# An LSTM kernel: a 256 KB reload split by partitions, and weight rows in DRAM reordered for strided stores

## The chip, the cores and the metric

One core of a Trainium2 chip. The metric is device time in microseconds of one execution; the kernel before is given by three runs with their median. Besides there is one profiled execution, whose own time is shown beside its span.

Engines in the text: PE (TensorE: matrix products; PEld its weight loads), DVE (VectorE), ACT (ScalarE), POOL (GpSimd), SP (SyncE, here only an issuer of DMAs). SPq and ACTq are the instruction queues of SP and ACT when they issue DMAs. Sixteen DMA engines carry out what both issue.

## What is computed

An LSTM over 512 steps with batch 32 and 512 hidden units, and its hidden states added to the input:

```
xW = einsum('ntd,dg->ntg', x, Wx) + b          # x: (32, 512, 512), Wx: (512, 2048)
for each step t:
    a = xW[:, t] + h @ Wh                      # Wh: (512, 2048)
    i, f, o = sigmoid(a[:, :512]), sigmoid(a[:, 512:1024]), sigmoid(a[:, 1024:1536])
    g = tanh(a[:, 1536:])
    c = f * c + i * g
    h = o * tanh(c)
    out[:, t] = x[:, t] + h
```

All in float32. The steps are sequential; `x @ Wx` is not.

## The kernel before

**Layout.** A step's gates stand as 128 partitions x 512 columns: partition `32 j + b` has block j of the hidden units for batch row b, and the 512 columns are two halves (`HW` = 256) of four gates x 64 units. `bank_of(t)` is the PSUM bank in which step t's gates are summed.

**A step** (the loop over `t`, line 779). `h_part(t)` puts `h @ Wh` into the bank: 16 products of 512 columns, which PE carries out as 32 matmul instructions (line 214). Then `cell(t)`: ACT takes the sigmoids and tanh (lines 228 to 230), DVE multiplies and adds (231 to 235), ACT takes tanh of c (237), DVE forms h and transposes it (239, 245) for the next step; POOL adds x (250) and SP stores pairs of steps (254). While the cell runs, PE works on `x @ Wx` of later steps. The bank of step t+1 is filled ahead by `seed_step` (line 591): ACT copies the ready `xW` rows from `xw`, a ring of three tiles, into the bank. `load_xw(t + 3)` reloads that ring from DRAM, from `kept` (line 575, steps 5 to 23) or from `xwd` (line 580, all groups): 128 partitions x 512 columns, 256 KB, by one DMA whose source is read with the index j outermost.

**The stream.** Steps 0 to 23 (the head) get their `xW` by plain products (`plain_block`, line 162), and so do the last 8. The 480 steps between are done in 20 groups of 24 steps, by a scheme with fewer products: sums of blocks of x (`u_op`, line 394) times sums of blocks of Wx, 20 slots a group, each slot with seven products `r` of a 2x2 scheme, each product four matmuls (line 483). Results are collected from PSUM by `evacuate` (ACT 529, 538, 545; DVE 535, 539, 542), combined by `w_op` (DVE 359) and stored to `xwd` in DRAM (`store_blocks`, line 375), from which the reload takes them. The work of a step is fixed when the program is made: 560 matmuls a group over 24 steps.

**Weight rows.** The sums of Wx blocks are the same for all groups. In the head DVE makes them: `tail_sums` once (lines 611 to 614), then `v_add` per slot (line 631) into one of six buffers, and `v_store` (line 645) sends them to `vdram` in DRAM. In `vdram`, row n holds the seven weight blocks (128 partitions x 256 columns each) that the stream uses together. They belong to different slots: `ROW` lists product and delay, so `(6, 1)` means that row n has product 6 of slot n-1. `RIGHT` gives a product's place in the row, `LEFT` its place among the x blocks. A slot's sum is thus spread over the rows s to s+3, and row numbers are taken modulo 20. `load_v` (line 557; 560 and 563 for the first and last rows) brings one row of 896 KB into `vring`, a ring of three, and `load_v_ahead` keeps two rows ahead of the products.

**Order.** The schedule is written by hand, and each engine's queue runs in that order. On SP a step has: the output store (which waits for POOL), the `xwd` stores (which wait for DVE), every eighth step a load of x, the `xw` reload, the rows of `vring` (which wait for PE to be done with the ring's place), and once per group `load_group` (1.5 MB of x). On ACT, in the head, the stores of `v_store` are issued in `flush_v`, after `cell(t)` and ahead of `seed_step(t + 1)`.

`late_load` (line 169) brings Wx back for the last 8 steps; `_laid_out` orders the inputs in memory before the run.

Of the kernel before, what the change touches and what calls it, by code (L numbers as in the profile page):

```python
# [7 lines left out]
F32 = mybir.dt.float32  # L8
# [4 lines left out]
P = 128  # L13
B = 32
T = 512
NJ = 4
G = 4
TC = 8
NCHUNK = T // TC
H = P // 2  # L20
W = G * P
HW = G * H
# [5 lines left out]
R = 20  # L28
TAU = (1, 0, 2)
NS = NG * R  # L30
# [27 lines left out]
]  # L58
BIAS_OF = {1: "b3", 3: "b1-b3", 8: "b2+b3", 11: "b2-b0", 13: "b0", 17: "b1-b0"}

ROW = ((1, 0), (5, 0), (2, 0), (6, 1), (3, 1), (7, 2), (4, 3))
LEFT = {1: 0, 2: 1, 4: 2, 5: 3, 6: 4, 7: 5, 3: 6}
RIGHT = {1: 0, 2: 1, 3: 2, 5: 3, 6: 4, 7: 5, 4: 6}

FILL = 107.0
PROD = 4 * 108.0
# [22 lines left out]
def kernel(  # L89
# [10 lines left out]
    nc = tc.nc  # L100
# [4 lines left out]
    dram = ctx.enter_context(tc.tile_pool(name="dram", bufs=1, space=DRAM))  # L105
# [7 lines left out]
    r1 = const.tile([P, 8, 4, HW], F32, name="r1")  # L113
    cbuf = const.tile([P, NC, 4, HW], F32, name="cbuf")
    r2 = cbuf[:, 0:8]
    wh_sb = const.tile([P, NJ, NJ, W], F32, name="wh_sb")
    vring = const.tile([P, 3, 7, HW], F32, name="vring")
# [8 lines left out]
    bias_full = const.tile([P, W], F32, name="bias_full")  # L126
    xw = const.tile([P, 3, W], F32, name="xw")

    vdram = dram.tile([R, P, 7, HW], F32, name="vdram")
    xwd = [dram.tile([6, P, NJ, W], F32, name=f"xwd_{i}") for i in range(2)]  # L130
    kept = dram.tile([HEAD - KEPT, P, W], F32, name="kept")

# [18 lines left out]
    def plain_block(t, c, bank):  # L151

        ko, ki = divmod(c, 2)
        for j in range(NJ):
            w = raw(ko * 4 + j)
            dst = bank[j * B : (j + 1) * B]
            if ki == 1:
                pieces = [(dst, w[:, 2:4].rearrange("p s c -> p (s c)"))]
            else:
                pieces = [(dst[:, 0:HW], w[:, 1]), (dst[:, HW:W], w[:, 0])]  # L160
            for n, (d, m) in enumerate(pieces):
                nc.tensor.matmul(  # L162
                    d, x_of(t)[:, c], m, start=c == 0 and n == 0, stop=True, skip_group_check=True
                )
# [109 lines left out]
    def flat(a):  # L274
        return a.rearrange("p a b -> p (a b)")
# [276 lines left out]
    def load_v(row):  # L552

        rr = row % R
        if row >= 3:
            if row < NS:
                nc.sync.dma_start(out=vring[:, row % 3], in_=vdram[rr])
            else:
                for a in {0: 2, 1: 5, 2: 6}[row - NS],:
                    nc.sync.dma_start(out=vring[:, row % 3, a:7], in_=vdram[rr, :, a:7])  # L560
            return
        for a, b in {0: ((0, 2), (3, 4)), 1: ((0, 5),), 2: ((0, 6),)}[row]:
            nc.sync.dma_start(out=vring[:, row % 3, a:b], in_=vdram[rr, :, a:b])

    def load_v_ahead():

# [5 lines left out]
    def load_xw(t):  # L572
        dst = xw[:, t % 3]
        if t < HEAD:
            nc.sync.dma_start(out=dst, in_=kept[t - KEPT])
            return
        g, n = divmod(t - HEAD, GS)
        assert getattr(group(g), "stored", 0) >= 4 * (n // 8 + 1), (t, group(g).__dict__.get("stored"))
        m, q = divmod(n, 4)
        nc.sync.dma_start(out=dst, in_=xwd[g % 2][m, q * B : (q + 1) * B].rearrange("b j c -> j b c"))  # L580

    xw_late = {}

    def seed_step(t):
# [10 lines left out]
    vroom = [vring[:, i] for i in range(3)] + [  # L595
        ubuf[:, 2 * i : 2 * i + 2].rearrange("p a b c -> p (a b c)").rearrange("p (k c) -> p k c", k=7) for i in range(3)
    ]
    free_v = list(range(6))
    vt = {}
# [5 lines left out]
    def tail_sums(a, b):  # L605

        z, w = r1[:, a:b], r2[:, a:b]
        b12, b11, b21, b22 = (z[:, :, i] for i in range(4))
        t1, t2, t3, n4 = (w[:, :, i] for i in range(4))
        return [  # L610
            lambda: sub(t1, b12, b11),
            lambda: sub(t3, b22, b12),
            lambda: sub(t2, b22, t1),
            lambda: sub(n4, b21, t2),
        ]

    def v_parts(i):
        if i < 8:
            return r1[:, i, 1:4], r2[:, i]
        return vroom[vt[i]][:, 0:3], vroom[vt[i]][:, 3:7]  # L620

    def v_add(terms):
        (a, sa), (b, sb) = sorted(terms.items(), key=lambda v: -v[1])
        op = add if sb > 0 else sub
        dst = free_v.pop(0)
        if a > 7 and b > 7:
            op(flat(vroom[dst]), flat(vroom[vt[a]]), flat(vroom[vt[b]]))
        else:
            for n, (pa, pb) in enumerate(zip(v_parts(a), v_parts(b))):
                d = vroom[dst][:, 0:3] if n == 0 else vroom[dst][:, 3:7]  # L630
                op(flat(d), flat(pa), flat(pb))
        for i in (a, b):
            v_used(i)
        return dst
# [5 lines left out]
                free_v.append(vt[i])  # L640

    def v_store(s, parts, whole=None):
        lo, hi = parts
        to = lambda k: vdram[(s + k) % R]
        dma = lambda o, i: nc.scalar.dma_start(out=o, in_=i)
        dma(to(0)[:, 0:2], lo[:, 0:2])
        dma(to(0)[:, 3], hi[:, 0])
        if whole is None:
            dma(to(1)[:, 2], lo[:, 2])
            dma(to(1)[:, 4], hi[:, 1])  # L650
        else:
            dma(to(1)[:, 2:5:2], whole[:, 2:5:2])
        dma(to(2)[:, 5], hi[:, 2])
        dma(to(3)[:, 6], hi[:, 3])

    def v_sum(i):
        if i > 7 and i not in vt:
# [4 lines left out]
    def v_slot(s):  # L662

        terms = V_OF[s]
        for i in terms:
            v_sum(i)
        if len(terms) > 1:
            d = v_add(terms)
            v_stores.append(lambda: v_store(s, (vroom[d][:, 0:3], vroom[d][:, 3:7]), vroom[d]))
            free_v.append(d)  # L670
        else:
            (i,) = terms
            parts = v_parts(i)
            v_stores.append(lambda: v_store(s, parts, vroom[vt[i]] if i > 7 else None))
            v_used(i)

    v_stores = []
# [39 lines left out]
    with tc.manual_schedule():  # L717
# [4 lines left out]
        for c in range(4):  # L722
            ko, ki = divmod(c, 2)
            nc.sync.dma_start(
                out=r1[:, 4 * ko : 4 * ko + 4, 2 * ki : 2 * ki + 2].rearrange("p j s c -> p j (s c)"),
                in_=wx[c].rearrange("p (j c) -> p j c", j=NJ),
# [178 lines left out]
def _laid_out(name, a):  # L905
    import numpy as _np

    if name == "x":
        a = a.reshape(B, NCHUNK, TC, NJ, NJ, B).transpose(1, 3, 5, 2, 4, 0).reshape(NCHUNK, P, TC * P)
    elif name == "x_grouped":  # L910
        a = a[:, HEAD : HEAD + NG * GS]
        a = a.reshape(B, NG, 3, 2, 4, NJ, 2, 2, B)[:, :, [TAU.index(m) for m in range(3)]]
        a = a.transpose(1, 5, 8, 2, 6, 3, 7, 4, 0)
        a = a.reshape(NG, P, 3, 2, 4, 4, B)[:, :, :, :, [2, 0, 1, 3]]
        a = a.reshape(NG, P, 6 * 4 * P)
    elif name == "cond_1024":
        a = a.reshape(B, NJ, NJ, B).transpose(1, 3, 2, 0).reshape(P, P)
    elif name == "L0_cond_Wx":
        a = a.reshape(NJ, NJ, B, G, NJ, 2, H).transpose(1, 0, 2, 4, 5, 3, 6).reshape(4, P, NJ, 2, HW).copy()
        a[0::2] = a[0::2, :, :, ::-1].copy()  # L920
        a = a.reshape(4, P, NJ * W)
    elif name == "L0_cond_Wh":
        a = a.reshape(NJ, NJ, B, G, NJ, 2, H).transpose(0, 2, 1, 4, 5, 3, 6).reshape(P, NJ * NJ * W)
    else:
        a = a.reshape(G, NJ, 2, H).transpose(1, 2, 0, 3).reshape(NJ, W)
    return _np.ascontiguousarray(a)
# [25 lines left out]
```

## Time and profile before

| | |
|---|---|
| runs | 3340.66, 3340.87, 3352.6 us, median 3340.87 |
| profiled execution | 3353.58 us, its span 3351.7 us |
| granted PE clock, mean | 0.977 |
| h products (line 214, the gate banks), 16288 matmuls | 1872.6 us busy, 41.9 idle before them |
| stream products on x sums (line 483), 14400 matmuls | 1107.1 us busy, 100.2 idle before them |
| PE waiting for `vring` (longest 6.0 us) | 97.3 us, 33 times |
| ACT's line 591 waiting for `xw` (longest 4.0 us) | 94.3 us, 38 times |
| SP waiting for PE before line 557 (longest 6.0 us) | 392.6 us, 150 times |

An x after a number is a count. Share of busy time is an average over the whole span; the prediction goes by stretches of it. In a timeline a line has start, duration, engine, line of the code, operation, what is written and read, shape and count; behind it in brackets the idle time before it and what ended it. In the rows for one line of the code, the three numbers are shortest, median and longest duration in ns.

### The profile page before, as it was taken

The page shows a single profiled execution, that of the slowest core. Times are in us where ns is not written, and L with a number is a line of the kernel's source. Part 1 is how long each engine was busy: PE and PEld are TensorE (multiplying, and loading weights), DVE is VectorE, ACT ScalarE, POOL GpSimd, SP SyncE. Part 2 cuts the span into 40 slices and gives each one's busy share as a digit, 9 for nine tenths or more (in the row PEclk, how much of TensorE's full clock was granted, in tenths as well). Part 3 has the DMA queues.
Part 4 walks back from the last instruction along what each step waited for, and adds up shares of the span by engine and source line. Part 5 has one row for each costly group of instructions (what it writes and reads, how often), then busy time and mean ns, then how long its engine had stood idle before and what let it go on. Part 6 is the DMA issues. An engine that isn't in the chain of part 4 may idle for free. (4 is left out here: it accounts for less than half of the span.)

```text
span 3351.7 us, 101512 instructions
## 1 busy us (share of the span) xinstructions
PE 3193.8 (95%) x41432; PEld 1856.8 (55%) x41432; DVE 2149.2 (64%) x6749; ACT 1350.9 (40%) x4525; POOL 233.0 (7%) x508
## 2 busy tenths in 40 slices
PE   8699999999999999999999999999999999999898
PEld 5355555555556555555556565555656565556454
DVE  5367667676666767576666666575766666666544
ACT  0144434444444444344434344444434443444344
POOL 0000000000000000000000000000000000000010
PEclk9799999999999999999999999999999999999999
DMA  7577676777677677767777676777677776767721
GB/s 281 194 275 257 215 251 230 233 240 236 234 236 245 216 258 227 237 225 234 247 231 242 219 254 215 249 232 234 229 238 243 233 247 213 254 219 252 230 101 40
DMA packets 277889, 766.46 MB, mean 229 GB/s; under 512 B 20656, under 2 KB 66736, under 8 KB 276912
## 3 DMA queue, kind: packets, MB, share of 16 engines
q1 hardware_dynamic: 259936, 740.83, 67.0%
q10 hardware_dynamic: 17488, 19.14, 1.7%
q8 instruction: 327, 5.36, 0.7%
q14 instruction: 138, 1.13, 0.1%
HBM read 577.18 MB, written 182.71 MB: 227 GB/s over the span
## 5 line engine op out<-in xcount | busy, mean ns | idle before, releaser
L214 PE MATMUL gbank<-wh_sb,ht 128*32 128x512 f32 (+1 forms) x16288 | 1872.6, 589 | 41.9 <-ACT gbank L591 34.0
L483 PE MATMUL xbank<-vring,ubuf 128*32 128x256 f32 x14400 | 1107.1, 384 | 100.2 <-DMA vring<-vdram 96.6
L214 PEld LDWEIGHTS gbank<-wh_sb,ht 128*32 128x32 f32 x16288 | 714.5, 111 | 879.1 <-issue 713.1
L483 PEld LDWEIGHTS xbank<-vring,ubuf 128*32 128x32 f32 x14400 | 712.3, 111 | 375.7 <-issue 238.9
L231 DVE TENSOR_TENSOR fc<-s 128x128 f32<-128x128 f32 (+1 forms) x546 | 153.5, 281 | 985.5 <-ACT s L228 984.6
L228 ACT ACTIVATE s<-gbank 128x256 f32<-128x256 f32 (+1 forms) x509 | 191.5, 376 | 1334.0 <-PE gbank L214 1178.9
L359 DVE TENSOR_TENSOR cbuf<-cbuf 128x1024 f32<-128x1024 f32 x480 | 577.3, 1217 | 2.1
L250 POOL TENSOR_TENSOR oc<-xnat,ht 128x128 f32<-128x128 f32 x504 | 232.8, 462 | 3080.3 <-DVE ht L245 1777.8
L591 ACT COPY gbank<-xw 128x512 f32<-128x512 f32 x473 | 282.2, 597 | 136.8 <-DMA xw<-xwd 94.3
L237 ACT ACTIVATE tanh_c<-s 128x64 f32<-128x64 f32 x1024 | 210.5, 249 | 270.6 <-DVE s L235 269.7
L529 ACT COPY cbuf<-xbank 128x512 f32<-128x512 f32 x400 | 231.3, 578 | 144.7 <-PE xbank L483 134.6
L239 DVE TENSOR_TENSOR hbuf<-o,tanh_c 128x64 f32<-128x64 f32 x1024 | 193.3, 225 | 140.3 <-ACT tanh_c L237 140.0
L483 PE MATMUL bbank<-vring,ubuf 128*32 128x256 f32 x2400 | 279.9, 384 | 1.2 <-DVE cbuf L535 1.2
L483 PE MATMUL xbank<-vring,r 128*32 128x256 f32 x2400 | 221.4, 379 | 1.2 <-ACT tanh_c L237 1.2
L483 PE MATMUL xbank<-vring,xs 128*32 128x256 f32 x2400 | 217.4, 380 | 2.7 <-ACT xbank L513 1.0
L245 DVE STREAM_TRANSPOSE ht<-hbuf 128x64 f32<-128x64 f32 x1022 | 193.7, 225 | 9.0 <-DVE hbuf L239 2.0
L235 DVE TENSOR_TENSOR s<-fc,ig 128x64 f32<-128x64 f32 x1024 | 183.9, 218 | 2.3
L233 DVE TENSOR_TENSOR ig<-s 128x64 f32<-128x64 f32 x1024 | 183.5, 218 | 0.0
L535 DVE TENSOR_TENSOR cbuf<-bbank,cbuf 128x256 f32<-128x256 f32 x400 | 163.7, 409 | 9.6 <-ACT cbuf L529 6.9
L539 DVE TENSOR_TENSOR cbuf<-xbank,cbuf 128x256 f32<-128x256 f32 x400 | 161.2, 403 | 4.8 <-ACT cbuf L538 3.1
L542 DVE TENSOR_TENSOR cbuf<-xbank,cbuf 128x256 f32<-128x256 f32 x400 | 161.7, 404 | 2.8 <-PE xbank L483 2.8
L545 ACT COPY cbuf<-xbank 128x256 f32<-128x256 f32 x400 | 147.6, 369 | 33.4 <-PE xbank L483 29.0
(84 smaller groups left out, 1817.0 us busy)
## 6 DMA issues: line engine op xcount, KB each, us to landing
vring<-vdram SPq DMA_DIRECT2D x397, 896.0 KB
xwd<-cbuf SPq DMA_DIRECT2D x240, 512.0 KB
xw<-xwd SPq DMA_DIRECT2D x480, 256.0 KB
out_dram<-oc SPq DMA_DIRECT2D x255, 128.0 KB
xnat<-in_x_dram SPq DMA_DIRECT2D x63, 512.0 KB
xs<-in_x_grouped_dram SPq DMA_DIRECT2D x10, 1536.0 KB
r<-in_x_grouped_dram SPq DMA_DIRECT2D x10, 1536.0 KB
kept<-cbuf SPq DMA_DIRECT2D x19, 256.0 KB
```

The source lines that it names most:

```text
L214: nc.tensor.matmul(dst[j * B : (j + 1) * B], state["ht"][:, k], m, start=False, stop=True, skip_group_check=True)
L228: nc.scalar.activation(s[:, i, 0:2], g[:, :, 0:2], AF.Sigmoid)
L233: nc.vector.tensor_mul(ig[:, u], s[:, u, 0], s[:, u, 2])
L235: add(nxt[:, u, 3], fc[:, u], ig[:, u])
L237: nc.scalar.activation(tanh_c[:, HALVES[u]], nxt[:, u, 3], AF.Tanh)
L239: nc.vector.tensor_mul(hbuf[:, HALVES[u]], o[:, u], tanh_c[:, HALVES[u]])
L245: nc.vector.transpose(ht[:, 2 * u : 2 * u + 2].rearrange("p q b -> p (q b)"), hbuf[:, HALVES[u]])
L250: (nc.gpsimd if t < T - 8 else nc.vector).tensor_add(oc[:, tt % 2], x_of(t), ht)
L359: op(c_of(dst), c_of(src), c_of(bb))
L483: nc.tensor.matmul(dst[q * B : (q + 1) * B], left_of(gr, s, r)[:, q * B : (q + 1) * B], vring[:, row % 3, RIGHT[r]], start=start, stop=Tru ...
L529: nc.scalar.copy(t[:, 0:4:3], xb.rearrange("p (n c) -> p n c", n=2))
L591: nc.scalar.copy(bank_of(t), src)
```

## The change

Three things. The reload of `xw` from `xwd` becomes four DMAs of 32 partitions, one per block j. The products of a row are ordered by delay (`ROW`, `RIGHT`: two places of delay 0, two of delay 1, two of delay 2, one of delay 3), so that a slot's sum lies in `vdram` at a constant stride and is stored by two DMAs, or three where the sum is a plain block of Wx. For that `vdram` has three rows more instead of the wrap by modulo, and `load_v` reads the rows 0, 1 and 2 of a pass in two parts. The sums are laid out in the buffers to match: `split_parts` takes places 0, 2, 4, places 1, 3, 5 and place 6, so `v_add` has three operations where a plain block of Wx is among its terms. The halves of the Wx blocks are stored in the reverse order in memory, and `plain_block` always uses two products of 256 columns.

```diff
-ROW = ((1, 0), (5, 0), (2, 0), (6, 1), (3, 1), (7, 2), (4, 3))
+ROW = ((1, 0), (5, 0), (6, 1), (3, 1), (7, 2), (2, 2), (4, 3))
 LEFT = {1: 0, 2: 1, 4: 2, 5: 3, 6: 4, 7: 5, 3: 6}
-RIGHT = {1: 0, 2: 1, 3: 2, 5: 3, 6: 4, 7: 5, 4: 6}
+RIGHT = {1: 0, 5: 1, 3: 2, 6: 3, 2: 4, 7: 5, 4: 6}
...
-    vdram = dram.tile([R, P, 7, HW], F32, name="vdram")
+    vdram = dram.tile([R + 3, P, 7, HW], F32, name="vdram")
...
-            if ki == 1:
-                pieces = [(dst, w[:, 2:4].rearrange("p s c -> p (s c)"))]
-            else:
-                pieces = [(dst[:, 0:HW], w[:, 1]), (dst[:, HW:W], w[:, 0])]
+            pieces = [(dst[:, 0:HW], w[:, 2 * ki + 1]), (dst[:, HW:W], w[:, 2 * ki])]
...
     def load_v(row):
 
         rr = row % R
-        if row >= 3:
-            if row < NS:
-                nc.sync.dma_start(out=vring[:, row % 3], in_=vdram[rr])
-            else:
-                for a in {0: 2, 1: 5, 2: 6}[row - NS],:
-                    nc.sync.dma_start(out=vring[:, row % 3, a:7], in_=vdram[rr, :, a:7])
-            return
-        for a, b in {0: ((0, 2), (3, 4)), 1: ((0, 5),), 2: ((0, 6),)}[row]:
-            nc.sync.dma_start(out=vring[:, row % 3, a:b], in_=vdram[rr, :, a:b])
+        cut = min(2 * rr + 2, 7)
+        parts = []
+        if row < NS:
+            parts.append((rr, 0, cut))
+        if row >= R and cut < 7:
+            parts.append((rr + R, cut, 7))
+        for n, a, b in parts:
+            nc.sync.dma_start(out=vring[:, row % 3, a:b], in_=vdram[n, :, a:b])
...
-        nc.sync.dma_start(out=dst, in_=xwd[g % 2][m, q * B : (q + 1) * B].rearrange("b j c -> j b c"))
+        for j in range(NJ):
+            nc.sync.dma_start(out=dst[j * B : (j + 1) * B], in_=xwd[g % 2][m, q * B : (q + 1) * B, j])
...
-        b12, b11, b21, b22 = (z[:, :, i] for i in range(4))
+        b12, b11, b22, b21 = (z[:, :, i] for i in range(4))
...
     def v_parts(i):
         if i < 8:
-            return r1[:, i, 1:4], r2[:, i]
-        return vroom[vt[i]][:, 0:3], vroom[vt[i]][:, 3:7]
+            return r1[:, i, 1:4], r2[:, i, 0:3], r2[:, i, 3]
+        return split_parts(vroom[vt[i]])
+
+    def split_parts(v):
+        return v[:, 0:5:2], v[:, 1:6:2], v[:, 6]
...
-            for n, (pa, pb) in enumerate(zip(v_parts(a), v_parts(b))):
-                d = vroom[dst][:, 0:3] if n == 0 else vroom[dst][:, 3:7]
-                op(flat(d), flat(pa), flat(pb))
+            for d, pa, pb in zip(split_parts(vroom[dst]), v_parts(a), v_parts(b)):
+                op(d, pa, pb)
...
     def v_store(s, parts, whole=None):
-        lo, hi = parts
-        to = lambda k: vdram[(s + k) % R]
         dma = lambda o, i: nc.scalar.dma_start(out=o, in_=i)
-        dma(to(0)[:, 0:2], lo[:, 0:2])
-        dma(to(0)[:, 3], hi[:, 0])
+        rows = vdram.rearrange("r p k c -> p r (k c)")
+
+        def skewed(a, n):
+            first = rows[:, s : s + 1, a * HW : (a + n) * HW]
+            return bass.AP(
+                tensor=first.tensor,
+                offset=first.offset,
+                ap=[first.ap[0], [P * 7 * HW + 2 * HW, 3], [1, n * HW]],
+            )
+
         if whole is None:
-            dma(to(1)[:, 2], lo[:, 2])
-            dma(to(1)[:, 4], hi[:, 1])
+            dma(skewed(0, 1), parts[0])
+            dma(skewed(1, 1), parts[1])
         else:
-            dma(to(1)[:, 2:5:2], whole[:, 2:5:2])
-        dma(to(2)[:, 5], hi[:, 2])
-        dma(to(3)[:, 6], hi[:, 3])
+            dma(skewed(0, 2), whole[:, 0:6].rearrange("p (d k) c -> p d (k c)", d=3))
+        dma(vdram[s + 3, :, 6], parts[2])
```

More of the change, by code (lines that the diff above doesn't have):

```diff
@@ L668, in v_slot @@
             d = v_add(terms)
-            v_stores.append(lambda: v_store(s, (vroom[d][:, 0:3], vroom[d][:, 3:7]), vroom[d]))
+            v_stores.append(lambda: v_store(s, split_parts(vroom[d]), vroom[d]))
             free_v.append(d)
@@ L918, in _laid_out @@
     elif name == "L0_cond_Wx":
-        a = a.reshape(NJ, NJ, B, G, NJ, 2, H).transpose(1, 0, 2, 4, 5, 3, 6).reshape(4, P, NJ, 2, HW).copy()
-        a[0::2] = a[0::2, :, :, ::-1].copy()
-        a = a.reshape(4, P, NJ * W)
+        a = a.reshape(NJ, NJ, B, G, NJ, 2, H).transpose(1, 0, 2, 4, 5, 3, 6)[:, :, :, :, ::-1].reshape(4, P, NJ * W)
     elif name == "L0_cond_Wh":
```

## The prediction

> **What bounds the kernel now.** I read the page first, then the busy time by stretch of the run, the waits, the landing times of the DMAs in the trace, and the timelines of the stretches that lose time.
>
> ```profile
> span 3351.7 us, 101512 instructions
> PE 3193.8 (95%) x41432; PEld 1856.8 (55%) x41432; DVE 2149.2 (64%) x6749; ACT 1350.9 (40%) x4525; POOL 233.0 (7%) x508
> ...
> DMA packets 277889, 766.46 MB, mean 229 GB/s; under 512 B 20656, under 2 KB 66736, under 8 KB 276912
> ...
> q1 hardware_dynamic: 259936, 740.83, 67.0%
> ```
>
> PE is the bound. What can be saved is its 158 us of idle time and the half-clock stretches that follow idle. The stretches (duration, PE busy, ..., granted clock, DMA share, GB/s) show where:
>
> ```profile
> 30.00:150.00 120.00, 85.97 (x964) 42.97 (x960) 63.84 (x130) 10.87 (x43) 3.65 (x8) 0.84 0.69 239
> 277.00:3025.00 2748.00, 2655.26 (x33971) 1563.58 (x33967) 1817.46 (x5706) 1152.06 (x3778) 198.23 (x432) 0.98 0.72 235
> 3025.00:3190.00 165.00, 151.60 (x1918) 88.53 (x1912) 99.53 (x322) 65.41 (x217) 12.51 (x25) 0.96 0.72 233
> ```
>
> In the steady stretch the first cell multiply (line 231) starts at 276.6 us in step 20 and at 3025.3 in step 452: 6.363 us a step. Undisturbed steps (under 6.15 us) average 6.005. The excess is 432 x 0.358 = 154.5 us, which agrees with 92.7 us of PE idle plus about 2% of 2748 us lost to the clock. It comes once per group of 24 steps:
>
> ```profile
> 322.46 0.59 ACT L591 COPY gbank<-xw 128x512 f32<-128x512 f32 x1 [1.51 <-DMA xw<-xwd]
> 330.24 0.59 ACT L591 COPY gbank<-xw 128x512 f32<-128x512 f32 x1 [3.37 <-DMA xw<-xwd]
> 336.23 1.94 PE L483 MATMUL xbank<-vring,ubuf 128*32 128x256 f32 x16 [4.44 <-DMA vring<-vdram]
> ```
>
> Both reloads are late, and the 16 matmuls after the stall take 1.94 us where an undisturbed 16 take 0.86: half clock.
>
> Why are they late? Every landed DMA puts one 4-byte packet per engine it used. 1526 transfers from SP and 109 from ACT at 16 engines each would give 26,160; with 256 data packets of 256 B that is 26,416 under 512 B. The page has 20,656, short by 5760 = 480 x 12. So each of the 480 transfers xw<-xwd (outer dimension 4) runs on 4 engines, and everything else on 16, the four 32-partition bias loads included. Their 480 x 256 KB = 125.8 MB put 31.5 MB on each of four engines; the other 615 MB put 38.4 MB on each of 16. At the mean rate (740.83 MB in 67.0% of 16 x 3351.7 us: 20.6 GB/s an engine) the four are 101% busy, the other twelve 56%. Landing times agree: in the steady stretch a reload lands 10.6 us after issue (median), a vring row 10.9; yet xw<-kept, the same 256 KB into the same tile on 16 engines, lands in 2.6 to 3.4 us in the head. A group load of 1.5 MB then meets four engines with no slack, and the backlog lasts beyond the two steps for which reloads are issued ahead.
>
> **Part 1, four reloads.** Each piece has outer dimension 32 on both sides, as the bias loads have, so I take 16 engines. The reload's share falls to 7.9 MB per engine, 46.3 in all: 67% busy, everywhere alike. With a third free, a group load (1.5 MB/16 at 20.6 GB/s: 4.8 us) is worked off in about 14 us, and rows should land in 4 to 6 us. Gain 154.5 us in full; I leave 0.25 us a group, so 150. Bounds: nothing (if the queues as a whole are the limit) to 154.5. In the last group (3025:3190) 13.4 us of idle and 4% of 165 us of clock make 20; there 1 MB weight loads arrive too, so 12, between 0 and 20.
>
> Cost: three more issues a step on SP.
>
> ```profile
> L580 SPq DMA_DIRECT2D xw<-xwd x480: 509/537/2123, 276.0 to 3296.1; - x160
> ...
> L729 SPq DMA_DIRECT2D bias_full<-in_L_cond_b_dram x4: 417/420/2421, 4.8 to 8.2; - x4
> ```
>
> 4 x 0.42 - 0.54 = 1.14 us a step. SP's issues are busy 680 us of those 432 steps, 1.58 a step, so it goes to 2.7 of 6.0. Behind the pieces queue the row load of line 557 and the xwd stores; PE waits for the row. The row is issued 1.1 us later but lands 5 us sooner: nothing. Without that cover it would be up to 1.1 us in five of six steps. ACT's line 591 waits for four landings instead of one: three 17 ns semaphore rows, before an idle of 2.7 us (wait for PE): nothing, 0.05 us a step if it were bare. PE and DVE gain no instruction.
>
> [...]
>
> **Part 2, stores of weight sums.** The page's 30:150 stretch loses 34.0 us of idle plus 16% of 120 us of clock: 53. The chain: ACT issues the stores of line 645 ahead of line 591, which PE needs.
>
> ```profile
> 79.16 5.09 ACTq L645 DMA_DIRECT2D vdram<-ubuf  x9
> ...
> 85.79 1.46 ACTq L645 DMA_DIRECT2D vdram<-cbuf  x3
> 87.29 2.86 ACTq L645 DMA_DIRECT2D vdram<-vring  x5
> 90.20 0.59 ACT L591 COPY gbank<-xw 128x512 f32<-128x512 f32 x1 [11.16 <-DMA vdram<-vring]
> ...
> 90.84 1.94 PE L214 MATMUL gbank<-wh_sb,ht 128*32 128x512 f32 x8 [13.15 <-ACT gbank L591]
> ```
>
> Before: 14 slots x 5 + 6 x 6 = 106 stores, about 0.5 us each. After: 14 x 2 + 6 x 3 = 46. One has 3 runs per partition; no row shows it, the nearest are the two-run stores (about 0.5) and 6-run group loads (0.59): 0.55, bounds 0.33 and 0.8. The burst above is 21 stores in 11.3 us (from 78.79), then 9 in 5. PE gaps: 13.15 goes, since two plain blocks (6.9 us) cover it; the 10.86 and 9.43, behind one plain block of 3.45, keep about 4 each (cell 2.2, stores 4.8, copy 0.6, less 3.45). That saves 25 idle and a few of clock: 28. Bounds: 53; and a loss of 26 if the hand-built pattern makes each store wait for the one before (46 x 2.05 us, the quickest landing of a store, against 68 us of bursts now).
>
> **Part 3, the rest.** Fourteen sums become three DVE operations instead of two: 256 columns more as their own instruction (0.41) less what the wide one shrinks (1217 - 949 ns): 14 x 0.14 = 2 us, hidden, since DVE is busy 63.8 of 120 us there; 2 if bare. Plain blocks trade one 512-column product for two of 256: a plain block already takes 3.45 us, and 256-column products stream at 16 in 0.86 us, the same per column: nothing; weight loads are covered by this stream, and bare would cost 8 x 2 x 0.054 us for each of 32 blocks, 28. Product 2 moves from third to sixth in a row: the shortest way from a product to one that needs its bank stays 8 products, over the 5.8 of a step, and evacuations keep their number: nothing, bounds plus and minus 5. Rows 0, 1, 2 of a pass load in two parts: 56 more issues x 0.42 = 24 us on SP in its idle time; bare, 24.
>
> **Sum**, against the profiled execution's 3353.58 us (span 3351.7 and 1.9 around it): 3353.6 - 150 - 12 - 28 = 3163.6, say 3164. Two of the three runs shown are 12.7 us under the profiled one. I take these as fewer stalls, the very time that goes, and subtract nothing more; against the median 3340.87 it is -5.3%.
>
> **Rivals.**
> A, part of the stalls stays: groups still collide, because 64 KB pieces at some partitions run slower or SP comes late. For it: late-issued rows exist (SP's line 557 waits 393 us for PE). Against: row loads have two rows of lead. Half of 150 back: 3239.
> B, the pieces don't spread, or the queues as a whole are the limit: then only parts 2 and 3 work: 3353.6 - 28, about 3326, and about 3313 against the median. Against: the bias loads and xw<-kept.
> C, slower: every DMA in the trace waits for the semaphore that it will raise, and eight serve both queues, so eight are in flight at most. SP now issues 3.0 a step; after, 6.13 (3 pieces and 0.13 row parts more). The cap decides from a mean landing of 8 x 6.005 / 6.13 = 7.8 us. If pieces keep the reload's 10.6 us and the rest falls to 5, the mean is 8.65 and a step 6.63 us: 456 steps x 0.625 = +285, 3449. For it: today's mean is 9.3 us. Against: that mean is made by four full engines; xw<-kept needs about 3.
>
> **How the numbers follow.** Forecast 0.70, with its own range 3125 (all 154.5, 20 and 53 saved: 3126) to 3215 (stores no gain, 24 us of SP bare). A 0.10, B 0.09, C 0.09, 0.02 for no change. The range goes up to A with the stores' gain halved and the row loads' 24 bare, 3277, say 3275; left out are B, C and no change. Measurements tell 0.5% from no change: faster 0.88 (forecast, A, nearly all of B), same 0.03, slower 0.09.
>
> **What would show it.** Packets under 512 B: (3022 + 49) x 16 + 256 = 49,392 if all spread; 23,040 fewer if pieces stay on four. PE's wait for vring and ACT's for xw fall from 97 and 94 us to under 10 each; steps stay at 6.0; the steady clock is 1.00. In 30:150, 46 stores on ACT, PE idle near 9 us. I am wrong if landings stay near 10 us, if SP's DMAs wait for their semaphores, or if undisturbed steps grow.

## The result and the profile after

The changed kernel takes 3188.84 us (median of four runs, 3187.78 to 3190.49); the kernel before, run beside it, 3346.28 us (3340.66 to 3352.6). The ratio is 0.953, its 95% interval 0.951 to 0.955. The forecast was 3164, with a range of 3125 to 3275. The profiled execution of the changed kernel took 3188.77 us, so profile stands against profile with 3353.58 - 3188.77 = 164.8 us, where the prediction's sum had 190.

The page's first part, its DMA packets and SP's queue, after:

```profile
span 3186.9 us, 104607 instructions
PE 3140.8 (99%) x41944; PEld 2017.6 (63%) x41944; DVE 2161.1 (68%) x6763; ACT 1344.6 (42%) x4525; POOL 233.3 (7%) x508
...
DMA packets 310997, 766.64 MB, mean 241 GB/s; under 512 B 49392, under 2 KB 92144, under 8 KB 310000
...
q1 hardware_dynamic: 296800, 740.82, 71.7%
```

PE's idle time fell from 158 us to 46. The packets under 512 B are 49,392, the very number that the prediction gave for reloads on 16 engines. The queue's time as a share of 16 engines rose from 67.0% to 71.7%, but mostly because the span is shorter: 67.0% of 3351.7 is 2246 us an engine, 71.7% of 3186.9 is 2285. All DMAs together cost 1.7% more engine time, spread over engines that had it to spare.

The same stretches as before (duration, PE busy, PEld, DVE, ACT, POOL, granted clock, DMA share, GB/s), the steady one ended earlier because the run is shorter:

```profile
30.00:150.00 120.00, 103.45 (x1528) 67.77 (x1531) 71.15 (x167) 14.97 (x57) 4.56 (x10) 0.94 0.71 246
...
277.00:2960.00 2683.00, 2680.39 (x34938) 1747.14 (x34932) 1874.34 (x5863) 1178.54 (x3885) 203.97 (x444) 1.00 0.77 248
```

In the steady stretch PE idles 2.6 us of 2683 and its clock is full; before it idled 92.7 of 2748 at 0.98. The head has improved, but 16.6 us of idle and a clock of 0.94 are left in it.

The waits (who waits for what: us in total, times, longest):

```profile
DVE cbuf L536 <- ACT cbuf L535: 70.4, 230, 1.6
...
ACT gbank L588 <- DMA vdram<-cbuf: 16.4, 2, 9.3
...
PE xbank L480 <- DMA vring<-vdram: 5.2, 2, 2.9
```

Line 480 here is line 483 before, 588 is 591, 642 is 645, 535 and 536 are 538 and 539. PE's wait for `vring` went from 97.3 us to 5.2, and ACT's wait for `xw` (94.3) is gone from the list. New is the first line: before, DVE waited 3.1 us in all for that copy. It is the trace of something that the prediction had put at nothing.

The landing times, last number of each line in the page's DMA part:

```profile
vring<-vdram SPq DMA_DIRECT2D x340, 896.0 KB, 5.9
xwd<-cbuf SPq DMA_DIRECT2D x240, 512.0 KB, 6.5
xw<-xwd SPq DMA_DIRECT2D x1920, 64.0 KB, 3.5
```

Before, a row took 10.9 us and a reload 10.6 (medians of the steady stretch, from the times at which the DMAs' semaphores rose).

Where the 164.8 us came from, by the start of the cell's first multiply in steps 20, 452 and 477, in us:

| stretch | before | after | gained | forecast |
|---|---|---|---|---|
| to step 20 (head) | 276.6 | 262.1 | 14.5 | 28 |
| steps 20 to 452 (steady) | 2748.6 | 2610.2 | 138.4 | 150 |
| steps 452 to 477 (last group) | 168.1 | 157.0 | 11.2 | 12 |
| step 477 to the last cell's multiply | 154.2 | 153.9 | 0.3 | 0 |

Two gaps are to be explained: 13.5 us in the head, 11.6 in the steady stretch. A steady step takes 6.042 us on average. Before, undisturbed steps averaged 6.005. In nearly every group of 24 steps after there are two of 6.31 us, 12 apart, and one of 6.18. A step of 6.31, first DVE, then ACT (start, duration, line, what is written and read; in brackets the idle time before it and its releaser):

```profile
312.34 0.42 DVE L536 TENSOR_TENSOR cbuf<-xbank,cbuf 128x256 f32<-128x256 f32 x1 [0.46 <-ACT cbuf L535]
312.68 0.41 DVE L539 TENSOR_TENSOR cbuf<-xbank,cbuf 128x256 f32<-128x256 f32 x1
313.01 1.08 DVE L391 TENSOR_TENSOR ubuf<-r 128x896 f32<-128x896 f32 x1
314.01 2.48 DVE L356 TENSOR_TENSOR cbuf<-cbuf 128x1024 f32<-128x1024 f32 x2
316.41 0.28 DVE L228 TENSOR_TENSOR fc<-s 128x128 f32<-128x128 f32 x1
```

```profile
311.45 0.59 ACT L526 COPY cbuf<-xbank 128x512 f32<-128x512 f32 x1
311.93 0.39 ACT L535 COPY cbuf<-xbank 128x256 f32<-128x256 f32 x1
...
315.70 0.39 ACT L225 ACTIVATE s<-gbank 128x256 f32<-128x256 f32 x1 [2.90 <-PE gbank L211]
```

DVE stands 0.46 us until ACT has copied product 3 (line 535), because ACT copies products 1 and 5 first (line 526). DVE then has 1.7 us of work in lines 536, 539 and 391 and two operations of line 356. The next cell's first sigmoid ends at 316.09, but `fc` starts at 316.41: the cell, which PE's next products need, is late by 0.3 us. PE's idle time hardly shows this: a matmul's row is 0.38 us long where the next one starts 0.05 us later, so that a pause like the one here (a start at 317.81, the next at 318.20) still counts as busy.

The head, ACT and its queue in the burst that the prediction showed:

```profile
75.81 0.37 ACTq L642 DMA_DIRECT2D vdram<-ubuf  x1
...
76.22 3.05 ACTq L642 DMA_DIRECT2D vdram<-ubuf  x3
79.31 1.28 ACTq L642 DMA_DIRECT2D vdram<-r  x1
80.62 2.58 ACTq L642 DMA_DIRECT2D vdram<-cbuf  x2
83.24 2.05 ACTq L642 DMA_DIRECT2D vdram<-vring  x2
85.34 0.59 ACT L588 COPY gbank<-xw 128x512 f32<-128x512 f32 x1 [9.28 <-DMA vdram<-cbuf]
```

These are the 9 stores that replace 21. The first takes 0.37 us, the others about one us each: 9.5 us in all, where the 21 took 11.3 and the forecast said 5. Both bursts carry 3.67 MB. PE's wait behind this burst, 13.15 us before and expected to go, is shorter but still there:

```profile
85.98 5.39 PE L211 MATMUL gbank<-wh_sb,ht 128*32 128x512 f32 x32 [6.68 <-ACT gbank L588]
```

With two more, of 7.36 and 2.51 us, it makes up the 16.6 us of idle.

### The profile page after: what moved, and what is told of

It is laid out like the page before. It is cut to its first block, busy times and chain, and to the rows that moved or that the text cites. A ratio compares the mean times of both kernels' runs of the same rounds, so it can differ in the third digit from the quotient of the medians.

```text
span 3186.9 us, 104607 instructions
## 1 busy us (share of the span) xinstructions
PE 3140.8 (99%) x41944; PEld 2017.6 (63%) x41944; DVE 2161.1 (68%) x6763; ACT 1344.6 (42%) x4525; POOL 233.3 (7%) x508
## 2 busy tenths in 40 slices
DMA packets 310997, 766.64 MB, mean 241 GB/s; under 512 B 49392, under 2 KB 92144, under 8 KB 310000
## 3 DMA queue, kind: packets, MB, share of 16 engines
q1 hardware_dynamic: 296800, 740.82, 71.7%
## 4 chain that ended last, share of the span: by engine, by line
PE 83%; DVE 8%; DMA 4%; ACT 2%; issue 1%; SPq 1%; ACTq 1%; DVEq 0%
PE gbank L211 48%; PE xbank L480 26%; PE bbank L480 5%; DVE cbuf L356 3%; PE xbank L211 2%; PE xbank L159 2%; DVE ubuf L391 1%; DMA xw<-xwd 1%; ACT tanh_c L234 1%; DMA xs<-in_L_cond_Wx_dram 1%; DVE ig L230 1%; ACTq L642 1%; DVE fc L228 1%; DVE cbuf L536 1%; ACT cbuf L535 1%
## 5 line engine op out<-in xcount | busy, mean ns | idle before, releaser
L211 PE MATMUL gbank<-wh_sb,ht 128*32 128x512 f32 (+1 forms) x16288 | 1837.6, 581 | 24.0 <-ACT gbank L588 16.5
L211 PEld LDWEIGHTS gbank<-wh_sb,ht 128*32 128x32 f32 x16288 | 785.5, 110 | 749.7 <-issue 577.1
L480 PE MATMUL xbank<-vring,ubuf 128*32 128x256 f32 x14400 | 1159.6, 379 | 6.8 <-DVE cbuf L536 3.0
L480 PEld LDWEIGHTS xbank<-vring,ubuf 128*32 128x32 f32 x14400 | 790.8, 110 | 234.3 <-issue 124.7
L480 PE MATMUL xbank<-vring,r 128*32 128x256 f32 x2400 | 236.9, 379 | 0.2 <-ACT xbank L510 0.2
L480 PE MATMUL xbank<-vring,xs 128*32 128x256 f32 x2400 | 230.3, 381 | 2.9 <-DMA vring<-vdram 2.9
L536 DVE TENSOR_TENSOR cbuf<-xbank,cbuf 128x256 f32<-128x256 f32 x400 | 163.7, 409 | 70.6 <-ACT cbuf L535 70.4
L480 PEld LDWEIGHTS bbank<-vring,ubuf 128*32 128x32 f32 x2400 | 147.8, 110 | 45.1 <-issue 29.9
## 6 DMA issues: line engine op xcount, KB each, us to landing
xs<-in_x_grouped_dram SPq DMA_DIRECT2D x10, 1536.0 KB, 10.6
```

Source lines behind the costliest of these rows:

```text
L211: nc.tensor.matmul(dst[j * B : (j + 1) * B], state["ht"][:, k], m, start=False, stop=True, skip_group_check=True)
L480: nc.tensor.matmul(dst[q * B : (q + 1) * B], left_of(gr, s, r)[:, q * B : (q + 1) * B], vring[:, row % 3, RIGHT[r]], start=start, stop=Tru ...
L536: add(t[:, 1], xb[:, HW:W], t[:, 1])
```

## The experiments

Four theories were tried. Theory 1: the reload ran on four engines, and that alone made rows and reloads late. Theory 2: the steps of 6.3 us come from the new order of products, through DVE's wait. Theory 3: a store's issue is long because it waits for room behind the data already queued, and costs time because ACT issues it. Theory 4 came from the second experiment and is told there. Each run was compared with the kernel before on the same chip; ratios are with 95% intervals. The kernel before had medians of 3346 to 3361 us on these chips, so a few us between times from different chips decide nothing; where so little matters, stretches of the profiles are compared.

### The reloads alone

The kernel before with one hunk of the change:

```diff
-        nc.sync.dma_start(out=dst, in_=xwd[g % 2][m, q * B : (q + 1) * B].rearrange("b j c -> j b c"))
+        for j in range(NJ):
+            nc.sync.dma_start(out=dst[j * B : (j + 1) * B], in_=xwd[g % 2][m, q * B : (q + 1) * B, j])
```

> The kernel before with the four reloads alone; rows and stores as before. Theory 1 (four overloaded DMA engines made the stalls): the steady excess of 154 us and about 11 us in the last group go, the head stays (step 20 starts near 276 us): span near 3187 us, packets under 512 B near 20,656 + 1440 x 16 + 5760 = 49,456. Theory 2 says that the new steps of 6.31 us come from the new product order: none here, steady mean 6.005 us. Its rival (the 6.31 us steps come from the reloads' extra issues and landings): they are here too, steady mean 6.04 us, span near 3202. Rival to theory 1 (rows and stores have a share in the steady gain): span above 3230.

Measured: 3195.74 us (3191.85 to 3197.36), ratio 0.952 (0.950 to 0.954), 49,456 packets under 512 B. Two lines, a stretch of the steady part and the landing of a reload:

```profile
277.00:2860.00 2583.00, 2581.04 (x33756) 1657.79 (x33748) 1806.90 (x5668) 1147.17 (x3753) 197.59 (x429) 1.00 0.78 249
...
xw<-xwd SPq DMA_DIRECT2D x1920, 64.0 KB, 4.4
```

The steady part takes 2600.7 us (6.020 a step), which is 9.5 us less than with the whole change. The two steps of 6.31 in every group are not there; 14 of 432 steps stand at 6.15 to 7.61 us, 8 of them at the same place of a group, and cost 5.6 us together. So one edit of two lines brings 148 of the 154.5 us there, as theory 1 says, and the regular slow steps belong to the rest of the change. Whether it is the engines or the smaller pieces that help, this run can't tell; later ones do. Step 20 starts at 278.8 us, no sooner than before: the reloads do nothing for the head.

### The rest alone

The changed kernel with that hunk undone.

> The changed kernel with the one reload of before; rows and stores as changed. Theory 1: stalls on vring and xw come back, about 90 us each; the head's 14 us stay saved: 3320 to 3345 us. The 6.31 us steps are there in undisturbed stretches (theory 2) or gone (its rival). If the rows had a share in the steady gain: under 3300.

Measured: 3267.41 us (3265.34 to 3268.81), ratio 0.973 (0.971 to 0.976): 53 us under the expected stretch. The head gained less than forecast (step 20 at 267.3, 9.3 us sooner), but the steady step takes 6.193 us, not 6.36, although in the trace a reload still lands 10.7 us and a row 11.1 us after its issue. In this kernel's list of waits (total, times, longest) ACT waits oftener than before and PE half as long:

```profile
ACT gbank L587 <- DMA xw<-xwd: 77.0, 56, 2.9
PE xbank L480 <- DMA vring<-vdram: 48.8, 40, 6.1
```

and its steady stretch, in columns as above, is

```profile
277.00:2860.00 2583.00, 2532.77 (x32810) 1530.79 (x32806) 1761.61 (x5505) 1115.29 (x3649) 192.18 (x417) 1.00 0.74 242
```

The mean wait is 1.2 to 1.4 us, and 50 us of PE idle in this stretch leave the clock at 1.00. In the kernel before, PE's wait is 2.9 us on average and the clock 0.98. Theory 4: the rows 0 to 2 at the start hold 14 products before and 12 after, so each later row starts 8 matmuls earlier against the step. The time from a step's start, where its row is issued, to the first matmul on that row goes by turns, in matmuls: 56, 38, 42, 47, 52 before, 48, 53, 34, 39, 44 after, in cycles of six steps. I read the difference so: before, a short turn met the deepest backlog after the group load, and one long wait came of it; after, the same backlog is met by several short ones.

### The slow steps: whose product goes first

The changed kernel, where `evacuate` takes products that DVE alone collects (2 and 7) ahead of the others:

```diff
-        for slot, r in finished:
+        for slot, r in sorted(finished, key=lambda f: f[1] not in (2, 7)):
```

> The changed kernel, but in evacuate DVE's additions that need no copy of ACT's (products 2 and 7) are issued first. Theory 2 (DVE idles up to 0.46 us for ACT's copy of product 3, and in two steps of 24 ends 0.3 us late for the cell): steps of 6.31 us fall to about 6.02, steady mean 6.005 to 6.02, 8 to 16 us less: near 3176 us. Rival (they come from the reloads): 3189, steps of 6.31 as before.

Measured: 3181.61 us (3179.22 to 3183.66), ratio 0.948 (0.945 to 0.950). DVE's wait for ACT's line 535 fell from 70.4 to 26.2 us, the steps of 6.31 became 6.12, and the steady part takes 2601.3 us, within 0.6 us of the reloads alone. Theory 2 holds, though the edit was expected to bring some 5 us more, and steps of 6.12 stay.

### The stores on SP's queue

```diff
-        dma = lambda o, i: nc.scalar.dma_start(out=o, in_=i)
+        dma = lambda o, i: nc.sync.dma_start(out=o, in_=i)
```

> The changed kernel with the stores of weight sums issued by SP instead of ACT. Theory 3 (the stores are held up by full DMA queues, 768 KB each at about 390 GB/s, and ACT's line 588 waits behind them in its queue): PE's idle time of 16.5 us in 30 to 150 us nearly goes and with it the half clock: 15 to 22 us less, near 3170 us. Rival (the head waits for DMA throughput or for the sums on DVE, whoever issues): no change, 3189, or SP's reloads of kept rows come late: slower.

Measured: 3168.00 us (3166.62 to 3172.23), ratio 0.944 (0.941 to 0.947). The stretch of the head:

```profile
30.00:150.00 120.00, 114.82 (x1736) 77.78 (x1732) 79.71 (x188) 20.44 (x73) 4.99 (x11) 0.99 0.84 296
```

and two of the rows for the store's line in that kernel (shortest, median and longest in ns):

```profile
L642 SPq DMA_DIRECT2D vdram<-vring x16: 442/943/2212, 52.0 to 105.9; - x16
...
L642 SPq DMA_DIRECT2D vdram<-ubuf x12: 442/1072/1249, 65.2 to 98.9; - x12
```

On SP a store takes just as long to issue, but nobody waits behind it: step 20 starts at 241.4 us instead of 262.1, and the clock in the head is 0.99. The steady part is unchanged (2610.4 us). Theory 3 holds in the half that costs time, the place of the issue; that the issue waits for room was not shown.

### Product 2 third in the order of execution again

The stores on SP, and:

```diff
-ROW = ((1, 0), (5, 0), (6, 1), (3, 1), (7, 2), (2, 2), (4, 3))
+ROW = ((1, 0), (5, 0), (2, 2), (6, 1), (3, 1), (7, 2), (4, 3))
```

> The changed kernel with the stores on SP, and product 2 carried out third in a row again, as before the change, while its place in memory stays fifth (delay 2). Theory 2 (the order of the evacuations, not the layout in memory, makes the 6.31 us steps): all undisturbed steps at 6.006, as with the reloads alone; 432 x 0.036 = 15 us less than stores on SP alone (3168): near 3153 us. Rival (the delay of 2 itself, with the sum's bank cleared later, makes them): near 3168, steps of 6.31 stay.

Measured: 3163.25 us (3161.83 to 3166.64), ratio 0.943 (0.942 to 0.945); the steady part 2603.8 us. The steps of 6.31 became 6.20 and did not vanish. The new place of product 2 is most of the loss, not all of it.

### The rest alone, with the stream held back

The rest alone, its stream started 8 matmuls later against the steps, so that the rows' turns fall as in the kernel before:

```diff
-target = min(R * 7 * 4 + (t + 1 - STREAM0) * R * 7 * 4 // GS, 4 * len(items))
+target = min(R * 7 * 4 - 8 + (t + 1 - STREAM0) * R * 7 * 4 // GS, 4 * len(items))
```

and the same 8 in the three conditions that follow the stream's place (`after`, and the two for the group load).

> The changed rows and stores with the one reload, but the stream held back by 8 matmuls (2 products) everywhere, with the group loads' conditions moved likewise. Theory 4 (why rows alone gained 80 us in the steady part: rows 0 to 2 now have 2 products fewer, which moves the row starts against the steps; the row load with the least lead no longer comes when the backlog after a group load is greatest, so the one wait of 4.4 us, which costs the clock too, becomes several of about 1 us): the long wait is back, PE waits near 90 us for vring, clock near 0.98, about 3335 us. Rival (the two-part rows or the new order themselves relieve the DMA queues): stays near 3267.

Measured: 3326.23 us (3320.37 to 3329.5), ratio 0.991 (0.989 to 0.993), 59 us slower than without the shift. PE's wait for rows in this kernel:

```profile
PE xbank L480 <- DMA vring<-vdram: 94.1, 34, 5.8
```

The stretch has 86 us of PE idle at a clock of 0.98:

```profile
277.00:2860.00 2583.00, 2497.23 (x32052) 1474.45 (x32047) 1722.77 (x5384) 1087.92 (x3565) 186.82 (x408) 0.98 0.73 236
```

The wait is that of the kernel before (97.3, 33 times), the clock is 0.98 again, and a step takes 6.342 us. Theory 4 holds as far as the phase goes: with four-engine reloads eight matmuls of it are worth 59 us. Which row meets which backlog was not followed further.

### One reload, on 16 engines

The changed kernel, with `xwd` laid out so that the 256 KB of a reload are contiguous. The reload is one DMA again, and the store to `xwd` becomes four of 32 partitions:

```diff
-    xwd = [dram.tile([6, P, NJ, W], F32, name=f"xwd_{i}") for i in range(2)]
+    xwd = [dram.tile([6, NJ, NJ, B, W], F32, name=f"xwd_{i}") for i in range(2)]
...
-            nc.sync.dma_start(
-                out=xwd[gr.g % 2][2 * tau : 2 * tau + 2, :, j].rearrange("m p c -> p m c"),
-                in_=cbuf[:, buf].rearrange("p (m n) c -> p m (n c)", m=2),
-            )
+            for q in range(4):
+                nc.sync.dma_start(
+                    out=xwd[gr.g % 2][2 * tau : 2 * tau + 2, q, j].rearrange("m b c -> b m c"),
+                    in_=cbuf[q * B : (q + 1) * B, buf].rearrange("b (m n) c -> b m (n c)", m=2),
+                )
...
-        for j in range(NJ):
-            nc.sync.dma_start(out=dst[j * B : (j + 1) * B], in_=xwd[g % 2][m, q * B : (q + 1) * B, j])
+        nc.sync.dma_start(out=dst, in_=xwd[g % 2][m, q].rearrange("j b c -> (j b) c"))
```

> The changed kernel, but xwd in DRAM is laid out so that a step's rows are contiguous: one reload of 128 partitions again, now with outer dimension 128, and each store to xwd split into four of 32 partitions instead. Theory 1 (what counts is the number of engines, not the number of pieces): as fast as the four reloads, 3180 to 3195 us, PE's wait for vring under 10 us, reload landing in 3 to 6 us. Rival (small pieces help because they land one by one or interleave): stalls come back, over 3230.

Measured: 3186.41 us (3184.37 to 3188.03), ratio 0.950 (0.949 to 0.952), with the landings

```profile
vring<-vdram SPq DMA_DIRECT2D x340, 896.0 KB, 6.1
...
xw<-xwd SPq DMA_DIRECT2D x480, 256.0 KB, 4.1
```

The page has 37,872 packets under 512 B, which is 16 for each of the 480 reloads and 960 stores. One transfer on 16 engines is as good as four. The gain was the engines, not the pieces.

### Eight pieces

The changed kernel with eight reloads of 16 partitions and 32 KB a step.

```diff
-        for j in range(NJ):
-            nc.sync.dma_start(out=dst[j * B : (j + 1) * B], in_=xwd[g % 2][m, q * B : (q + 1) * B, j])
+        for i in range(2 * NJ):
+            j, b = divmod(16 * i, B)
+            src = xwd[g % 2][m, q * B + b : q * B + b + 16, j]
+            nc.sync.dma_start(out=dst[16 * i : 16 * i + 16], in_=src)
```

> The changed kernel with eight reloads of 16 partitions a step. SP issues 10.1 DMAs a step, 8 x 0.45 us for the reload alone, about 5.2 of 6.0 us busy; with eight semaphores the mean landing must stay under 8 x 6.0 / 10.1 = 4.75 us, and it is about 4.3 with four pieces. Theory of rival C's cap: it starts to bind, SP waits for DMA semaphores, row loads come late, steps grow: 3220 to 3400 us. Rival (queue time and semaphores still suffice): 3185 to 3195.

Measured: 3695.57 us (3686.11 to 3698.1), ratio 1.101 (1.099 to 1.104). What SP's queue waited for, and then PE (total, times, longest):

```profile
SPq L579 <- DMA vring<-vdram: 394.8, 343, 2.9
SPq L579 <- DMA xwd<-cbuf: 240.8, 205, 2.8
```

```profile
PE xbank L480 <- DMA vring<-vdram: 353.7, 122, 7.9
```

This is rival C's mechanism: a piece waits for the semaphore that it will raise, which an earlier row or store still holds. The time lies beyond the 3400 us expected for it, and the mechanism set in earlier than the rival's formula says. With 10.13 DMAs a step the mean landing that decides would be 8 x 6.005 / 10.13 = 4.7 us; the mean in this trace is 4.3, and a step takes 7.13 us. In the changed kernel's trace 3050 of 3071 DMAs wait for the semaphore that they raise (before, 1496 of 1635, not every one as the prediction has it), and the eight are taken in fixed turn: from 277 to 2860 us each of 2605 DMAs raises the one of the DMA eight places before it. So an issue waits for that DMA, whether or not others have landed. I read this as the eight being held up by the slowest transfer among them, not by the mean; no run tried that alone. SP's issues are also busy for 1721 of 2623 us with eight pieces, 66%; how much the issues alone would cost was not separated.

### Two pieces

The changed kernel with two reloads of 64 partitions, j outermost. One run, with its profile.

```diff
-        for j in range(NJ):
-            nc.sync.dma_start(out=dst[j * B : (j + 1) * B], in_=xwd[g % 2][m, q * B : (q + 1) * B, j])
+        for j in range(0, NJ, 2):
+            src = xwd[g % 2][m, q * B : (q + 1) * B, j : j + 2]
+            nc.sync.dma_start(out=dst[j * B : (j + 2) * B], in_=src.rearrange("b j c -> j b c"))
```

> The changed kernel with two reloads of 64 partitions, each read with j outermost (outer dimension 2), in place of four of 32 partitions. Theory 1 (a transfer runs on as many engines as its outermost dimension, and the single reload was late because that was 4): two engines a piece. Packets under 512 B: 1151 x 16 + 256 + 960 x 2 = 20,592. If it is the same two engines each time, they carry 125.8/2 + 38.4 = 101 MB each, at the 20.6 GB/s an engine that the kernel before shows 4.9 ms, at 26 GB/s 3.9 ms: 3900 to 4900 us, PE waiting for vring and ACT for xw for hundreds of us, TensorE clock well below 1. Rival (a reload is late because it is one large transfer, and smaller pieces in flight are what helps): 64 KB or 128 KB makes little difference, 3190 to 3240 us, 3071 - 960 transfers on 16 engines, 34,032 packets under 512 B.

Measured: 4471.24 us, a third slower than the kernel before (3361.16 on that chip). Its DMA packets, from the page:

```profile
DMA packets 282185, 766.43 MB, mean 171 GB/s; under 512 B 20592, under 2 KB 63344, under 8 KB 281200
```

The waits for rows and reloads, and then a stretch of the steady part:

```profile
PE xbank L480 <- DMA vring<-vdram: 797.8, 211, 9.5
...
ACT gbank L589 <- DMA xw<-xwd: 587.3, 189, 7.0
```

with PE busy for three quarters of it, the clock at 0.90 and the DMA share at 0.53:

```profile
277.00:2860.00 2583.00, 1968.49 (x23126) 1024.85 (x23122) 1239.29 (x3879) 794.37 (x2571) 134.22 (x294) 0.90 0.53 171
```

The packets are the 20,592 of two engines a piece. Half of the engines' time is unused, and yet PE starves. If it is the same two engines each time, they carry 125.8/2 + 38.4 = 101 MB each in 4471 us, 22.7 GB/s, between the mean of 20.6 before and the expectation's 26 (the median packet of 7168 B took 272 ns before, 26.4 GB/s): they would set the time. The trace does not name the engines; had the two pieces gone to different pairs, four engines would have carried the reloads, as in the rest alone, which took 3267 us. This is the strongest evidence for theory 1: smaller pieces made it worse, and fewer engines carried each.

### Together

Product 2 third, the DVE-first order in `evacuate`, and the stores on SP:

> The changed kernel with its stores on SP's queue, product 2 third in the order of execution, and evacuate taking products 2 and 7 (which DVE alone collects) ahead of the others. Theory 2 (the steps of 6.2 us that stayed with product 2 third are DVE waiting for ACT's copy of product 3): that wait falls from 31 us to near nothing, the steady steps 20 to 452 from 2603.8 to about 2600.7 us (6.020 a step, as with the reloads alone), 3159 to 3161 us. Rival (what is left of them is the order of the row itself, through a bank or a load): 2603 to 2604 us, 3163 us.

Measured: 3162.54 us (3160.8 to 3163.85), ratio 0.941 (0.939 to 0.943). The rival was right: no gain over the run without the DVE-first order, within their ranges. In the stretch from 277 to 2860 us both kernels' lists of waits have the same line:

```profile
DVE cbuf L536 <- ACT cbuf L535: 26.5, 71, 0.5
```

and both keep two steps of 6.20 us per group. In such a step of this kernel DVE takes product 2 first and then stands 0.37 us until ACT has copied product 3, behind two other copies (lines 542 and 526); DVE's own order can't shorten that.

And the same with `xwd` laid out for one contiguous reload:

> As the run before, with xwd laid out so that a reload is one contiguous 256 KB transfer on 16 engines and its store is four transfers of 32 partitions. Theory 1: as fast as four pieces, within 3 us of the run before (the one-transfer layout alone was 2.4 us faster than the changed kernel), 3156 to 3163 us. Rival (pieces of 32 partitions cost something that the slack of the changed kernel hid): over 5 us faster, under 3155 us.

Measured: 3158.98 us (3157.43 to 3160.11), ratio 0.940 (0.938 to 0.942), the fastest of the study: 30 us under the changed kernel. It is 3.6 us under the run before it, 0.6 more than theory 1's bound and less than the rival's 5. In the two profiles 3.35 us of it lie in steps 452 to 476 (149.58 against 146.23 for the first 24), and the steady steps are nearly equal (6.028 and 6.024), so four pieces cost next to nothing where the queues are regular. The changed kernel and its one-reload variant differ in the same place (150.98 against 147.02); what costs it there was not followed.

## Why the prediction was right, and where it was off

**The bound and the cause.** Right. The four-engine reload was read from packet counts in the profile before; the counts after (49,392), with the reloads alone (49,456) and with two pieces (20,592) all follow from the same arithmetic; the trace after has 49,136 packets of 4 B, 16 for each of its 3071 DMAs. In the counts of packets under 512 B a reload's engines go with its outermost dimension: 4 ran on 4 engines (20,656 packets before), 2 on 2 (20,592), and 32, 128 and 16 on 16 (49,392, 37,872 and 80,112). No other dimension was tried. One reading that the prediction leaned on was too kind: xw<-kept lands in 2.5 to 3.5 us only until 160 us into the run; from 170 us on, beside the row loads, it took 4.7 to 8.2. It was weaker evidence than it seemed against one large transfer being slow as such; the run with one reload on 16 engines, which lands in 4.1, settles that.

**Part 1: 150 forecast, 148 measured alone** (2748.6 - 2600.7). The prediction left 0.25 us a group, 4.5 us in all; the slow steps that stay there cost 5.6. For the last group 12 were forecast, and 11.2 measured with the whole change. Landings of rows, 4 to 6 us forecast, are 5.9. The three further issues, costed at nothing, are nothing: after, SP's issues are busy 2.83 us a step (2.7 forecast), and PE waits for `vring` 1.5 us in the whole run with the reloads alone.

**Part 3: the step that failed is "Product 2 moves from third to sixth in a row ... nothing, bounds plus and minus 5".** I followed the way of a product to the next that needs its bank, but not which of two products finished together DVE takes first, nor whom it waits for. The cost is 9.5 us in the steady part (2610.2 against 2600.7), nearly twice the bound; two edits that undo it in different ways brought 8.9 and 6.6 us back there. Most of it is shown; the 0.2 us that stay in two steps a group with product 2 third are not resolved further than ACT's copies ahead of that of product 3. The 9.5 us are a difference: the reloads alone have slow steps of their own.

**Part 2: 28 forecast, 14.5 measured.** The count of stores (46) was right; the term that was mis-sized is "0.55, bounds 0.33 and 0.8" for one. The medians are 0.88 to 1.20 us. From the rows for the store's line after (shortest, median, longest in ns):

```profile
L642 ACTq DMA_DIRECT2D vdram<-vring x16: 366/876/1557, 55.0 to 120.3; - x16
L642 ACTq DMA_DIRECT2D vdram<-cbuf x12: 533/1202/2183, 53.6 to 126.4; - x12
...
DMA to landing us min/median/max: 2.9/5.6/8.0
```

The row from which I took 0.5 was a mean over stores of 128 and 256 KB at a moment when the queue already moved much: 21 stores of 3.67 MB in 11.3 us are 325 GB/s. Fewer, larger stores move the same bytes at 386. Costed by bytes rather than by count, the burst of nine would have been forecast at up to 11.3 us; it took 9.5. That reading is consistent with the traces; no run shows an issue time against the queue's fill alone. For the longer burst two plain blocks of 6.9 us were too little cover, and of PE's wait of 13.15 us, which was to go, 6.68 stayed. The chain itself, stores ahead of the copy that PE needs, was right: taken off ACT, the same stores cost 20.7 us less to step 20.

**The rivals.** A and B fall with the landings and the packet count. B's time, parts 2 and 3 alone, 3326, was tried: 3267. The step behind it that failed is the assumption that the stalls of four-engine reloads are the same whatever the rest does; they depend on a phase of eight matmuls, and with that phase restored it is 3326. The parts therefore don't add: -4.8% and -2.7% alone, -4.7% together, because both shorten the same stalls and the second also brings the slow steps. C did not come at 6.13 DMAs a step: their mean landing in the trace is 4.4 us, under the 7.8 that would decide. One of the prediction's own signs of being wrong, SP's DMAs waiting for their semaphores, does show, though only in short waits, above all behind a load of x:

```profile
SPq L577 <- DMA xnat<-in_x_dram: 47.2, 48, 2.5
```

In the steady stretch SP waits about 100 us for landings, and no row is late for it there: PE's waits for `vring` are two in the whole run, 5.2 us together. At 10.13 DMAs a step C came.

**The spread.** I took the 12.7 us by which two runs before were under the profiled one as fewer stalls, and subtracted nothing more. The runs after lie within 2.7 us, with the profiled one 0.1 us under their median, so this holds as far as it can be seen.

## What to carry to other kernels

A mean share of 16 engines can hide that a few of them set the time (67.0% before, by the prediction's estimate 101% on the reload's four): count the engines of each kind of transfer (the packets that end a transfer show it) and put a dimension that brings all 16 (here 16, 32 and 128 did, 2 and 4 did not) outermost on both sides before cutting it into pieces. The two bursts of stores here cost nearly the same for the same bytes, 11.3 us in 21 stores and 9.5 in 9, so keep such a burst off an engine whose next instruction PE waits for. When an order of work is changed for the memory's sake, follow what each engine does with two results that come at once; and don't add up the gains of parts that remove the same wait.

## What the hardware showed

- The number of engines decided: with the same bytes and otherwise the same kernel, reloads on 2 engines a piece give 4471 us, on 4 engines 3267, on 16 engines 3186 to 3189.
- The issue of a DMA is not a fixed cost: in the burst shown, stores took 0.37 us at the start and 1.0 to 1.3 on average behind others, and from SP's queue the same store took as long as from ACT's (medians 0.94 and 0.88).
- Eight semaphores, taken in turn, bound the DMAs of SP and ACT before their mean landing says so: at 10.13 a step, with a mean landing of 4.3 us where 4.7 would decide, SP waited 395 us for rows and 241 for stores, and the kernel took 3696 us instead of 3189. What part of this SP's longer issue time has is open.
- The clock went with the length of each wait: 50 us of idle in waits of 1.2 us on average left it at 1.00, 86 us in waits of 2.8 us brought 0.98, and after the stall of 4.44 us shown before, 16 matmuls took 1.94 us instead of 0.86. From 277 to 2860 us of the kernel before, the rest alone and the same held back, none of PE's 59 waits of 0.5 to 1.8 us is followed by a half clock; with 34 of the 39 waits of 2.3 to 5.9 us a stretch at 0.5 begins during the wait or within 4 us after it. The shortest wait that brought the half clock was 2.48 us.
